# A fused stencil, attention, MLP and expert kernel: two sets of sums go to GpSimd, and the experts' response moves to other slots

## The chip, the cores and the metric

The kernel runs on one core of a Trainium2 chip. The time is that of the whole program on the device in microseconds; of several runs the median is given. All arithmetic is float32. In the rows of the profile PE is TensorE (PEld its weight loads), DVE is VectorE, ACT is ScalarE, POOL is GpSimd, and SP is the engine that issues nearly all DMAs.

## What is computed

The reference is a chain of four stages on x of shape (8, 512, 512), cut here to what matters:

```python
x = max(x + df(x, A_grid, B_grid) * dt, 0)                  # L0: a stencil on a 512x512 grid
x = layernorm(x) * (1 + scale) + shift                      # L1: attention with 16 heads ...
x = x + (softmax(q @ k.T + bias, mask) @ v @ Wo + bo)
h = layernorm(x) * g2 + beta2
x = x + gelu(h @ W1 + b1) @ W2 + b2                         # ... and an MLP, 512 -> 2048 -> 512
e = expert_idx[b]                                           # L2: one expert for each sample
r = x + gelu(x @ Wi[e] + bi[e]) @ Wo[e] + bo[e]
x = layernorm(r) * gamma[e] + beta[e]
basis = gram_schmidt(U) @ gram_schmidt(V).T                 # L3: a low-rank response with a gate
strength = sigmoid(relu(mean(x) @ w1.T + b1) @ w2.T + b2) * sigmoid(safety)
out = x + strength * ((x @ basis) @ basis.T[:, :32] @ resp_w.T + resp_b + safety_bias)
```

## The kernel before

The grid stage and the attention take the first 1078 us and aren't touched. `mlp_stage` follows. It makes sixteen passes q = 0 to 15: q = 0 to 7 are the MLP of L1 for one sample each, q = 8 to 15 the expert of L2 for one sample each, with L3 for the sample before woven in. Each pass multiplies 512 rows by 512x2048 (layer 1, `wi`) and by 2048x512 (layer 2, `wo`).

**Two levels of Strassen-Winograd.** Every product is split in quadrants, and seven products of sums stand for eight. Layer 1 does so once: four groups g of the hidden units, seven products each (the table `L1`), from sums S1 to S4 of the weights (`w_quads`, GpSimd) and T1 to T4 of the features (`b_staged`, tiles `tb` and, in place, `bt`). They are used in the order B00, B10, T2, T3, T1, T4, B11. Layer 2 has seven products P1 to P7 of quarters of the activations (`act`, sums s1 to s4: `s13`, `s2`, `s4`) and of `wo` (sums t1 to t4: `t13`, `t2`, `t4`). P1 and P5 are taken whole (`second`, tile y). P2, P6, P7, P3 and P4 are split once more (`third`, tiles y_32a/b, y_40a/b, y_44a/b, y_48a/b and y_52a/b); their own sums are `l_sum` (left, from act, on DVE) and `r_sum` (right, from wo, on GpSimd).

**Slots.** A pass has 56 slots: four matmuls of 256 columns each in layer 1 (slots 0 to 27), in P1 (28 to 31) and in P5 (36 to 39), and seven matmuls of 128 columns in P2 (32 to 35), P6 (40 to 43), P7 (44 to 47), P3 (48 to 51) and P4 (52 to 55). The last pass has P3 ahead of P7. `at(hooks, s, f, ...)` puts a piece of work f in slot s; `go(s)` records it there. So hooks fix the order in which an engine's instructions stand, not their time: an engine runs ahead, or falls behind, as its inputs, its buffers and its own order let it. What is recorded through `pin` keeps the order of the program on its engine. The weight loads of `load_wi`, `load_wo`, `load_x` and `load_extra` go to SP's queue without `pin`, and a scheduler places them there; SP carries out its queue in order, and an issue that has to wait for a buffer holds up those behind it.

**Staging.** Where DVE would read both operands from SBUF, ACT first copies one of them to PSUM (`staged`, L1519 for one part and L1524 for two, tag "tr", two buffers); l_sum's parts are called p2a, p2b, p2c and so on. PSUM tiles of products have the tag "u" with six buffers, among them y, u, and po of the response.

**What the change touches**, with line numbers of the kernel before:

- `b_staged` (L1527), called in slot 51 for the next pass: T1, T2, T3 (in place of quadrant 01 of bt) and T4 on DVE, each in two halves of 128x256, with three staged copies of two halves each.
- `s4` and `s4_stage` (L1746, L1751): S4 = quadrant 01 of act minus S2, per group 128x512, on DVE from staged copies, in slots 38 to 40. S4 is the left side of P3 and overwrites the quadrant that P2 reads.
- `t4` (L1742): T4 of wo, on GpSimd, from slot 37 (q up to 8), 40 (q = 9 to 14) or 43 (q = 15). It is the right side of P4.
- the table of l_sum's and r_sum's slots (L1757): the columns are the name of the product, the slots of the left sums and the slots of the right sums.
- `add_beta` (L2079), for the sample o = q - 1, in slot 36: DVE adds strength times the response's bias to the row `beta` in place (L2081); then GpSimd adds that row to x, four adds of 128x512.
- `tail_sum` (L2085): the response's matmuls po, four of 512 columns with 32 rows each, in slot 46. `tail_add` (L2092): x += strength * po on DVE, in four slots; the output goes out after the second and the fourth.

Near it and unchanged: `load_extra` (L1391), in slot 45 for the next pass, loads that expert's rows, gamma and beta with two buffers each; the row of q + 1 takes the place of that of q - 1. `load_wi` (L1363) loads the next pass's first and second weight groups in slots 48 and 52, 1 MB each, into buffers that P7's and P3's sums have used. `gs_stage`, `gs_norm` and `gs_b` are a step of the Gram-Schmidt, in passes 0 to 8; the step at the end of passes 0 to 7 stands in slots 52, 53 and 55: DVE makes two dot products, GpSimd a root (gs_d), DVE updates the matrix (qm), and GpSimd issues two DMAs (qb<-qm, L1259).

Of the kernel before, what the change touches and what calls it, by code (L numbers as in the profile page):

```python
# [16 lines left out]
ALU = mybir.AluOpType  # L17
# [1180 lines left out]
def mlp_stage(tc, a, small, xp, io, wo8, x1d, ident, eidx, sigs, layernorm, rstd_of, phalf, wl3, g2, b1, first):  # L1198
    nc = tc.nc
    H = 256  # L1200
    NG = 4
    pin = tc.keep_in_program_order
    with ExitStack() as ctx:
# [12 lines left out]
        def add(out, x, y, op=ALU.add):  # L1216
            pin(nc.vector.tensor_tensor(out, x, y, op))  # L1217
# [9 lines left out]
        n = 2 * RK  # L1227
# [299 lines left out]
        def b_staged(q):  # L1527
            def b(i, k, j):
                v = bts[q][2 * i + k]
                return v[:, 2 * j : 2 * j + 2, :, :] if len(v.shape) == 4 else v[:, H * j : H * j + H]  # L1530

            t1, t2, t4 = (
                as_rows(ap.tile([P, 2, H], F32, name=f"tb{i}_{q}", tag=f"tb{i}", bufs=1), b(0, 0, 0))
                for i in range(3)
            )
            b01, b11 = (staged(f"b{i}1_{q}", b(i, 0, 1), b(i, 1, 1)) for i in range(2))
            for k in range(2):
                add(t1[k], b01[k], b(0, k, 0), ALU.subtract)
            for k in range(2):
                add(t2[k], b11[k], t1[k], ALU.subtract)  # L1540
            for k in range(2):
                add(b(0, k, 1), b11[k], b(0, k, 1), ALU.subtract)
            tbs[q] = {
                "B00": lambda k: b(0, k, 0), "B10": lambda k: b(1, k, 0),
                "B11": lambda k: b(1, k, 1), "T3": lambda k: b(0, k, 1),
                "T1": lambda k: t1[k], "T2": lambda k: t2[k],
                "T4": lambda k: t4[k],
            }
            b10 = staged(f"b10_{q}", b(1, 0, 0), b(1, 1, 0))

            def rest():
                for k in range(2):
                    add(t4[k], b10[k], t2[k], ALU.subtract)

            rest()

        def b_quads(q, hold=False):
            def b(i, k, j):
# [52 lines left out]
        def run(q, hooks):  # L1611
# [10 lines left out]
            def act_quad(g, i, j):  # L1622
                return acts[:, g, 2 * j : 2 * j + 2, H * i : H * i + H]

            def stage(key, src):
                st[key] = staged(f"{q}_{key}", src)

            st = {}
# [114 lines left out]
                o = quad(wo[:, g], 1, 0)  # L1743
                gadd(o, o, quad(wo[:, g], 0, 0), sub)

            def s4(*gs_):  # L1746
                for g in gs_:
                    o = act_quad(g, 0, 1)
                    add(o, st[f"s4_{g}"], act_quad(g, 0, 0), sub)

            def s4_stage(*gs_):  # L1751
                for g in gs_:
                    stage(f"s4_{g}", act_quad(g, 0, 1))

            tail, last = q > NB, q == NQ - 1
            four = (40, 41, 42), (44, 45, 46)
# [1 line left out]
                at(hooks, s, set_up, part)  # L1758
            for g in range(NG):
                at(hooks, 30 + g, t2, g)  # L1760
                at(hooks, (43 if last else 40 if tail else 37) + g, t4, g)
            for key, ss_, ts_ in (
                ("p2", (28, 29, 30), (23, 24, 25, 26) if q else (20, 21, 22, 23)),
                ("p6", (36, 37, 38), (33, 34, 35, 36)),
                ("s4", (), ()),
                ("p7", four[last], (28, 28, 29, 29) if tail else (19, 20, 21, 22) if q else (23, 24, 25, 26)),
                ("p3", four[not last], (43, 43, 44, 45) if tail and not last else (40, 41, 42, 43)),
                ("p4", (47, 48, 49), (46, 46, 47, 48) if tail else (44, 45, 46, 47)),
            ):
                if key == "s4":  # L1770
                    at(hooks, 30, stage, "s2_0", act_quad(0, 0, 0))
                    for g in range(NG):
                        at(hooks, 31 + g, s2, g)
                    at(hooks, 38, s4_stage, 0, 1)
                    at(hooks, 39, s4, 0, 1)
                    at(hooks, 39, s4_stage, 2, 3)
                    at(hooks, 40, s4, 2, 3)
                    continue
                if key == "p4" and last:
                    continue  # L1780
                for n_, s in enumerate(ss_):
                    at(hooks, s, l_sum, key, n_)
                for n_, s in enumerate(ts_):
                    at(hooks, s, r_sum, key, n_)
# [418 lines left out]
        def at(hooks, s, f, *args):  # L2203
            hooks.setdefault(s, []).append(lambda: f(*args))
# [8 lines left out]
        for q in range(NQ):  # L2213
            hooks = {}
            nx = q + 1 if q + 1 < NQ else None

            if q:
                at(hooks, 0, load_wi, q, 2)
                at(hooks, 0, load_wi, q, 3)
                at(hooks, 1, w_quads, q, 1, gadd)  # L2220
            at(hooks, 0, load_wo, q)
            if nx:
                if nx >= NB:
                    at(hooks, 45, load_extra, nx)
                at(hooks, 2, load_x, nx)
                at(hooks, 48, load_wi, nx, 0)
                at(hooks, 52, load_wi, nx, 1)
            if 1 <= q <= NB:
                at(hooks, 4, lambda q=q: nc.sync.dma_start(x2d[q - 1], xs[q - 1]))

            if q <= NB:
                done = 4 * q - 1 if q else 0
                rounds = [(5, 8)] if q == NB else [(5, 8), (13, 16), (21, 24), (52, 55)]
                if q == 0:
                    rounds = (6, 9), (14, 17), (52, 55)
                for i, (s, e) in enumerate(rounds):
                    at(hooks, s, gs_stage, done + i)
                    at(hooks, s + 1, gs_norm, done + i)
                    at(hooks, e, gs_b, done + i)
            for r in range(R):  # L2240
                at(hooks, (24 if q > NB else 9 if q else 10) + r, add_row, q, r)
            at(hooks, 8 if q else 7, w_quads, q, 2, gadd)
            at(hooks, 16 if q else 14, w_quads, q, 3, gadd)
            for g in range(NG):
                at(hooks, ((5, 6, 12, 13) if q else (10, 12, 17, 18))[g], t13, q, g)
            if nx:
                if nx < NB:
                    for h in range(2):
                        at(hooks, 17 + h if q else 19 + 2 * h, norm, nx, h)
                    for r in range(R):  # L2250
                        at(hooks, 33 + r, normed, nx, r)
                for r in range(R):
                    at(hooks, 34 + r, lambda r=r, n=nx: rows32(
                        n, r, hs[n, r] if n < NB else xs[n][:, r, :]
                    ))
                at(hooks, 38 if q <= NB else 40, turn, nx)
                if nx < NB:
                    for c in range(KC):
                        at(hooks, 46 + c, scale, nx, c)
                at(hooks, 51, b_staged, nx)  # L2260
                at(hooks, 51, w_quads, nx, 0, gadd)
            if q == 0:
                at(hooks, 1, gs_a, 0)
                at(hooks, 10, load_constants)
            if q == 1:
                at(hooks, 10, constants)
            if q == NB:
                for i, s in enumerate((10, 13, 15, 17, 20)):
                    at(hooks, s, low_rank, i)
            elif q > NB:  # L2270
                every = range(R)
                o = q - 1
                at(hooks, 5, tail_norm, o, every)
                at(hooks, 9, tail_normed, o)
                for r in range(R):
                    at(hooks, 11 + r, lambda r=r, o=o: rows32(o, r, xs[o][:, r, :]))
                at(hooks, 15, tail_spread, o)
                at(hooks, 18, tail_gamma, o, every)
                for c in range(KC):
                    at(hooks, 20 + c, tail_scale, o, c)  # L2280
                at(hooks, 25, tail_feats, o, every)
                at(hooks, 26, gate, o)
                at(hooks, 32, strength, o)
                at(hooks, 35, guarded, o)
                at(hooks, 36, add_beta, o)
                for r in range(R):
                    at(hooks, 46, tail_sum, o, r)
                    at(hooks, ((47, 49, 53, 54) if nx else (47, 48, 49, 51))[r], tail_add, o, r)
            if q == NQ - 1:
                half = range(0, 2)  # L2290
                at(hooks, 49, tail_norm, q, half)
                at(hooks, 50, tail_normed, q)
                for c in range(KC):
                    at(hooks, 52 + c, tail_turn, q, half, [c])
                at(hooks, 55, last_affine, 0)
            run(q, hooks)


# [86 lines left out]
```

## Time and profile before

| | |
|---|---|
| median of 3 runs | 2631.25 us (2630.48 to 2633.49) |
| the profiled execution | 2631.78 us; its span 2630.0 us, granted TensorE clock 0.994 |
| busy in the span | PE 98%, DVE 79%, POOL 66%, ACT 52% |
| pass q = 3, 1362.66 to 1456.08 | 93.42 us; PE busy throughout, DVE 77.40, POOL 72.34, ACT 40.90 |
| pass q = 10, 2025.42 to 2122.99 | 97.57 us; PE busy 97.26, DVE 74.67, POOL 71.45, ACT 42.95 |
| one add of 128x512 on POOL | 1277 ns |
| the same on DVE, one operand in PSUM | 680 ns, the next starts 600 ns after it |

How to read it: a pass begins with its first matmul u<-bt,wi. Line L1217 is every add of DVE in this stage and L1220 every one of POOL, so groups are told apart by their tiles: "act<-act,st_p4a" is P4's S3, "yw<-y_48a,yw" the evacuation of P3's first half, "x<-y_44b,x" the addition of P7 to x. A line of the waits names who waited, for whom, the sum of the waits, how often, and the longest. A line of the timeline gives start, duration, engine, line, operation, tiles, count, and in brackets the idle time of the engine ahead of it with what ended it.

### The profile page before, as it was taken

The page shows a single profiled execution, that of the slowest core. Times are in us where ns is not written, and L with a number is a line of the kernel's source. Part 1 is how long each engine was busy: PE and PEld are TensorE (multiplying, and loading weights), DVE is VectorE, ACT ScalarE, POOL GpSimd, SP SyncE. Part 2 cuts the span into 40 slices and gives each one's busy share as a digit, 9 for nine tenths or more (in the row PEclk, how much of TensorE's full clock was granted, in tenths as well). Part 3 has the DMA queues.
Part 4 walks back from the last instruction along what each step waited for, and adds up shares of the span by engine and source line. Part 5 has one row for each costly group of instructions (what it writes and reads, how often), then busy time and mean ns, then how long its engine had stood idle before and what let it go on. Part 6 is the DMA issues. An engine that isn't in the chain of part 4 may idle for free. (4 is left out here: it accounts for less than half of the span.)

```text
span 2630.0 us, 45403 instructions
## 1 busy us (share of the span) xinstructions
PE 2584.8 (98%) x16048; PEld 1967.7 (75%) x16048; DVE 2081.1 (79%) x4116; ACT 1366.7 (52%) x2871; POOL 1734.7 (66%) x1422
## 2 busy tenths in 40 slices
PE   6999999999999999999999999999999999999998
PEld 3455555555555555798899899899899989989887
DVE  7978898978888756588888888788778778777777
ACT  2676767677767766244344344343443543544443
POOL 4555565655555656378778777877767777777774
PEclk9999999999999999999999999999999999999999
DMA  8765757666767556443653653465345265255250
GB/s 325 259 225 189 256 194 249 211 220 226 248 212 250 178 158 203 143 148 79 175 181 60 164 197 100 105 190 154 100 168 186 89 207 191 82 201 196 77 177 33
DMA packets 242135, 460.69 MB, mean 175 GB/s; under 512 B 33936, under 2 KB 77528, under 8 KB 232822
## 3 DMA queue, kind: packets, MB, share of 16 engines
q1 hardware_dynamic: 238042, 447.04, 49.9%
q0 software_dynamic: 3552, 10.72, 4.2%
q8 instruction: 128, 2.10, 0.3%
q14 instruction: 97, 0.79, 0.1%
q10 hardware_dynamic: 316, 0.03, 0.0%
HBM read 398.43 MB, written 55.09 MB: 172 GB/s over the span
## 5 line engine op out<-in xcount | busy, mean ns | idle before, releaser
L998 POOL TENSOR_TENSOR bt<-bt,mk 128x1024 f32<-128x1024 f32 x256 | 542.0, 2142 | 59.0 <-DMA bt<-in_bias 37.6
L1026 ACT ACTIVATE bt<-bt,mn 128x512 f32<-128x512 f32 x512 | 365.8, 718 | 78.5 <-DVE mn L1021 78.3
L564 PEld LDWEIGHTS tr<-ident,bt 128*128 128x128 f32 x2048 | 229.6, 141 | 149.4 <-issue 102.4
L1021 DVE CUSTOM_DVE_ANT_0 bt<-s,bt 128x512 f32<-128x512 f32 x512 | 329.8, 683 | 4.3 <-PE s L561 3.6
L1211 PE MATMUL u<-bt,wi 128*128 128x256 f32 x1440 | 330.8, 379 | 0.0
L1052 ACT COPY pt<-tr 128x512 f32<-128x512 f32 x376 | 207.9, 584 | 209.2 <-PE tr L564 201.8
L1211 PEld LDWEIGHTS u<-bt,wi 128*128 128x128 f32 x1440 | 272.3, 190 | 36.4
L564 PE MATMUL tr<-ident,bt 128*128 128x128 f32 x2048 | 276.6, 277 | 7.5 <-ACT pt L1052 2.9
L1217 DVE TENSOR_TENSOR act<-u,u 128x512 f32<-128x512 f32 x256 | 172.6, 682 | 123.2 <-PE u L1211 70.8
L1211 PE MATMUL u<-tb,ws 128*128 128x256 f32 x1024 | 242.7, 380 | 0.0
L1220 POOL TENSOR_TENSOR wo<-wo 128x512 f32<-128x512 f32 x175 | 221.1, 1277 | 8.7
L1211 PEld LDWEIGHTS u<-tb,ws 128*128 128x128 f32 x1024 | 193.9, 190 | 27.7 <-DVE x L1217 1.4
L1050 DVE COPY pt<-tr 128x512 f32<-128x512 f32 x136 | 93.7, 689 | 140.5 <-PE tr L564 140.0
L1796 ACT ACTIVATE act<-act,bi 128x512 f32<-128x512 f32 x128 | 83.6, 711 | 222.7 <-DVE act L1217 222.6
L1796 ACT ACTIVATE act<-act,b 128x512 f32<-128x512 f32 x128 | 83.6, 711 | 192.8 <-DVE act L1217 192.8
L561 PE MATMUL s<-kt,qt 32*128 32x512 f32 x1024 | 167.5, 643 | 1.2 <-ACT kt L651 0.8
L1220 POOL TENSOR_TENSOR q<-wo 128x512 f32<-128x512 f32 x96 | 121.7, 1278 | 49.8 <-PE pf L1211 32.5
L1217 DVE TENSOR_TENSOR u<-u,u 128x512 f32<-128x512 f32 x192 | 130.5, 680 | 28.9 <-PE u L1211 28.3
L1220 POOL TENSOR_TENSOR ws<-wi 128x512 f32<-128x512 f32 x60 | 76.7, 1278 | 91.7 <-DMA wi<-in_W 49.9
L561 PE MATMUL ctx<-pt,v 128*32 128x256 f32 x2048 | 128.7, 390 | 0.0
L561 PEld LDWEIGHTS ctx<-pt,v 128*32 128x32 f32 x2048 | 63.0, 111 | 83.0 <-issue 49.3
L1220 POOL TENSOR_TENSOR q<-wo,q 128x512 f32<-128x512 f32 x96 | 122.6, 1277 | 2.7
(473 smaller groups left out, 5909.9 us busy)
## 6 DMA issues: line engine op xcount, KB each, us to landing
bt<-in_bias SPq DMA_DIRECT2D x256, 512.0 KB
wo<-in_W SPq DMA_DIRECT2D x32, 1024.0 KB
wi<-in_Wi SPq DMA_DIRECT2D x32, 1024.0 KB
wo<-in_Wo_e SPq DMA_DIRECT2D x32, 1024.0 KB
wi<-in_W SPq DMA_DIRECT2D x28, 1024.0 KB
td<-tt SPq DMA_DIRECT2D x22, 1024.0 KB
bt<-td SPq DMA_DIRECT2D x120, 128.0 KB
gq<-coef_q SPq DMA_DIRECT2D x21, 512.0 KB
```

Of the source, the lines that this page charges most:

```text
L561: pin(nc.tensor.matmul(out, lhsT=lhsT, rhs=rhs, start=start, stop=stop))
L564: pin(nc.tensor.transpose(out, src, ident))
L998: nc.gpsimd.tensor_tensor(bt, bt, mask[b, r][:, None, :].to_broadcast([P, 2, S]), ALU.add)
L1021: nc.vector.tensor_tensor_reduce(bt[:, i, :], ss[h], bt[:, i, :], -1.0, 3.0e38, ALU.add, ALU.min, mn)
L1026: nc.scalar.activation(bt[:, i, :], bt[:, i, :], AF.Exp, bias=mn, scale=-1.0, accum_out=sums[b, c][:, h, r : r + 1],)
L1050: pin(nc.vector.tensor_copy(pt[:, :, r % 2, :], tr))
L1052: pin(nc.scalar.copy(pt[:, :, r % 2, :], tr))
L1211: pin(nc.tensor.matmul(out, lhsT=lhsT, rhs=rhs, start=start, stop=stop))
L1217: pin(nc.vector.tensor_tensor(out, x, y, op))
L1220: pin(nc.gpsimd.tensor_tensor(out, x, y, op))
L1796: nc.scalar.activation(acts[:, g, k, :], acts[:, g, k, :], func, bias=bi[:, j : j + 1])
```

## The change

S4 is made on GpSimd, in place and without staging, one group in each of the slots 37 to 40 (36 to 39 in the last pass). The staging copies of S4 go. T4 of wo moves to slots 43 to 46 (45 to 48 in the last pass). P4's left sums move one slot forward, and some right sums of P3 and P4 in passes after 8 to other slots. The sums T3 and T4 of the next pass's features leave DVE: they are made on GpSimd in slot 55 from SBUF, and their staged copy goes. From q = 9 to 14 add_beta moves from slot 36 to 49, the four matmuls of tail_sum from 46 to 51, and tail_add from 47, 49, 53, 54 to 52, 53, 54, 55. In the last pass add_beta moves from 36 to 42.

```diff
 b_staged:
-            for k in range(2):
-                add(b(0, k, 1), b11[k], b(0, k, 1), ALU.subtract)
...
-            b10 = staged(f"b10_{q}", b(1, 0, 0), b(1, 1, 0))
 
             def rest():
                 for k in range(2):
-                    add(t4[k], b10[k], t2[k], ALU.subtract)
-
-            rest()
+                    gadd(b(0, k, 1), b(1, k, 1), b(0, k, 1), ALU.subtract)
+                for k in range(2):
+                    gadd(t4[k], b(1, k, 0), t2[k], ALU.subtract)
+
+            late[q] = rest
 run:
-            def s4(*gs_):
-                for g in gs_:
-                    o = act_quad(g, 0, 1)
-                    add(o, st[f"s4_{g}"], act_quad(g, 0, 0), sub)
-
-            def s4_stage(*gs_):
-                for g in gs_:
-                    stage(f"s4_{g}", act_quad(g, 0, 1))
+            def s4(g):
+                o = act_quad(g, 0, 1)
+                gadd(o, o, act_quad(g, 0, 0), sub)
...
-                at(hooks, (43 if last else 40 if tail else 37) + g, t4, g)
+                at(hooks, (36 if last else 37) + g, s4, g)
...
-                ("p3", four[not last], (43, 43, 44, 45) if tail and not last else (40, 41, 42, 43)),
-                ("p4", (47, 48, 49), (46, 46, 47, 48) if tail else (44, 45, 46, 47)),
+                ("p3", four[not last], (40, 40, 41, 42) if last else (40, 41, 42, 43)),
+                ("t4", (), ()),
+                ("p4", (46, 47, 48), (46, 46, 47, 48)),
...
-                    at(hooks, 38, s4_stage, 0, 1)
-                    at(hooks, 39, s4, 0, 1)
-                    at(hooks, 39, s4_stage, 2, 3)
-                    at(hooks, 40, s4, 2, 3)
+                if key == "t4":
+                    for g in range(NG):
+                        at(hooks, (45 if last else 43) + g, t4, g)
                     continue
 the passes:
                 at(hooks, 51, w_quads, nx, 0, gadd)
+                at(hooks, 55, lambda n=nx: late.pop(n)())
...
-                at(hooks, 36, add_beta, o)
+                at(hooks, 49 if nx else 42, add_beta, o)
                 for r in range(R):
-                    at(hooks, 46, tail_sum, o, r)
-                    at(hooks, ((47, 49, 53, 54) if nx else (47, 48, 49, 51))[r], tail_add, o, r)
+                    at(hooks, 51 if nx else 46, tail_sum, o, r)
+                    at(hooks, ((52, 53, 54, 55) if nx else (47, 48, 49, 51))[r], tail_add, o, r)
```

More of the change, by code (lines that the diff above doesn't have):

```diff
@@ L1548, in b_staged @@
             }
-            b10 = staged(f"b10_{q}", b(1, 0, 0), b(1, 1, 0))
             def rest():
                 for k in range(2):
-                    add(t4[k], b10[k], t2[k], ALU.subtract)
-            rest()
+                    gadd(b(0, k, 1), b(1, k, 1), b(0, k, 1), ALU.subtract)
+                for k in range(2):
+                    gadd(t4[k], b(1, k, 0), t2[k], ALU.subtract)
+            late[q] = rest
+        late = {}
         def b_quads(q, hold=False):
@@ L1764, in run @@
                 ("p6", (36, 37, 38), (33, 34, 35, 36)),
-                ("s4", (), ()),
+                ("s2", (), ()),
                 ("p7", four[last], (28, 28, 29, 29) if tail else (19, 20, 21, 22) if q else (23, 24, 25, 26)),
-                ("p3", four[not last], (43, 43, 44, 45) if tail and not last else (40, 41, 42, 43)),
-                ("p4", (47, 48, 49), (46, 46, 47, 48) if tail else (44, 45, 46, 47)),
+                ("p3", four[not last], (40, 40, 41, 42) if last else (40, 41, 42, 43)),
+                ("t4", (), ()),
+                ("p4", (46, 47, 48), (46, 46, 47, 48)),
             ):
-                if key == "s4":
+                if key == "s2":
                     at(hooks, 30, stage, "s2_0", act_quad(0, 0, 0))
@@ L1773, in run @@
                         at(hooks, 31 + g, s2, g)
-                    at(hooks, 38, s4_stage, 0, 1)
-                    at(hooks, 39, s4, 0, 1)
-                    at(hooks, 39, s4_stage, 2, 3)
-                    at(hooks, 40, s4, 2, 3)
+                    continue
+                if key == "t4":
+                    for g in range(NG):
+                        at(hooks, (45 if last else 43) + g, t4, g)
                     continue
```

## The prediction

> **What bounds the kernel.** I read the page's engine table first, then who waited for whom on PE, then the same for the DMA queue on SP, then the order of time of one pass.
>
> ```profile
> span 2630.0 us, 45403 instructions
> ...
> PE 2584.8 (98%) x16048; PEld 1967.7 (75%) x16048; DVE 2081.1 (79%) x4116; ACT 1366.7 (52%) x2871; POOL 1734.7 (66%) x1422
> ```
>
> PE is busy for all but 45 us. The waits of PE from 1000 us on (the last attention rows and all sixteen passes) show what is left to win:
>
> ```profile
> PE y_52a L1211 <- DVE act L1217: 2.6, 4, 0.8
> PE y_48a L1211 <- DVE yw L1217: 2.4, 7, 0.6
> PE y L1211 <- ACT act L1796: 0.8, 1, 0.8
> ```
>
> Only the first two touch what is moved. So no more than about 5 us (0.2%) can be won, while a new wait costs its length in each pass where it stands. A pass is 93.42 us in the first half (q = 2 to 4, no loss) and 97.57 us for q = 9 to 14. I work out one pass of each kind, in offsets (+) from its first layer-1 product: q = 3 from 1362.66 and q = 10 from 2025.42.
>
> **First half, q = 0 to 7.** S4 on GpSimd: 4 adds at 1.277 us, 5.1 us, in place of 4 staging copies (ACT) and 4 adds (DVE, one each 0.60 us). POOL comes to them at +62.8, P2 has been read by +61.5, so they end at +68.0; P3's sums are staged at about +77.6 on ACT. Hidden, with 9 us to spare. T4, which they displace, moves back 10.2 us to +78.1 and P4's sums to +83.2; P4 starts at +87.2. POOL has the room: it stands idle for 8.22 us before the next weights' sums.
>
> DVE's four S4 adds were behind P6's sums; without them DVE reaches the end of P6's product early and waits for PE: its addition to x ends at +77.0 instead of +77.9. P4's first sum now goes ahead of y_44b's evacuation and S3 is there at +84.4 (it was +87.7; PE wants it at +88.1): the y_52a waits go, **-2.6**.
>
> T3 and T4 of the next features leave DVE (4 x 0.33 = 1.3 us, there with PSUM copies) and go to the end of POOL's queue, behind the Gram-Schmidt DMAs that wait for DVE's qm. qm ended at +97.90; I get +96.28 (0.3 from the lead above, 1.3 from the sums gone). The DMAs start 0.53 later, as before, and take 1.03: T3 starts at +97.87. A POOL add of 128x256 isn't in the trace. Bounds: 0.64 us (half of 128x512 at 1.277) and 0.845 (the line through 1.277 and the 2.142 of 128x1024). I take 0.74, the line from 128x1 at 0.196 to 1.277. Halves at +98.6 and +99.3; PE's fourth product wants them at 93.42 + 3 x 1.727 = +98.60 and +99.03. A wait of 0.35 in six passes: **+2.1** (bounds 0.5 and 4; if DVE wins nothing, 1.9 us x 7 = 13). T4 is wanted 3.5 us after T3: no cost. POOL's lag of 1.7 us afterwards delays the last GELU by about as much as PE is delayed plus its slack of 1.3: no cost.
>
> [...]
>
> **Passes q = 9 to 14.** Here add_beta moves from slot 36 to 49, the quarter sums from 46 to 51. The load of the next expert's beta row (load_extra, slot 45) takes the buffer of the row that add_beta reads: two buffers, and the row of q+1 replaces that of q-1. In the built program's order this load still stands on SP's queue ahead of the next pass's first weights, and waits for the fourth POOL add of add_beta. That wait already exists:
>
> ```profile
> SPq L1368 <- PE y_44b L1211: 34.5, 6, 6.2
> ...
> SPq L1398 <- POOL x L1220: 23.5, 6, 3.9
> ```
>
> Today it is free, because SP then waits up to 6.2 us for wi's buffer anyway. SP and POOL in q = 10:
>
> ```profile
> 2097.37 0.33 SPq L1398 DMA_DIRECT2D beta<-in_beta  x1
> 2097.89 1.33 SPq L1402 DMA_DIRECT2D cols<-in_gamma  x1
> 2099.41 0.38 SPq L1402 DMA_DIRECT2D cols<-in_beta  x1
> ...
> 2103.70 0.43 SPq L1409 DMA_DIRECT2D x<-x2d  x1
> 2110.13 0.40 SPq L1368 DMA_DIRECT2D wi<-in_Wi  x1
> ```
>
> ```profile
> 2092.38 4.97 POOL L1220 TENSOR_TENSOR x<-x,beta 128x512 f32<-128x512 f32 x4 [4.24 <-DVE beta L2081]
> ...
> 2115.28 1.27 POOL L1220 TENSOR_TENSOR ws<-wi 128x512 f32<-128x512 f32 x1 [1.40 <-DMA wi<-in_Wi]
> ```
>
> The reader is to see: the adds end at 2097.35, the beta load goes out at 2097.37; wi goes out at 2110.13 and is there at 2115.28, 5.15 us later. PE wants it at 2122.99, so 7.7 us are spare. In the new order nothing but the two cols loads lies between beta and wi: 2.6 us from the end of add_beta (2097.35 to 2099.79, and 0.15 to the next issue). So wi lands 2.6 + 5.15 = 7.75 after add_beta's end.
>
> When is that? DVE's rows:
>
> ```profile
> 2103.33 0.57 DVE L1217 TENSOR_TENSOR y_40b<-y_40b,yw 128x384 f32<-128x384 f32 x1 [0.39 <-ACT y_40b L1886]
> 2103.93 0.70 DVE L1217 TENSOR_TENSOR y_40b<-y_40b,yu 128x512 f32<-128x512 f32 x1
> 2104.66 0.69 DVE L1217 TENSOR_TENSOR x<-y_40b,x 128x512 f32<-128x512 f32 x1
> 2106.61 0.69 DVE L1217 TENSOR_TENSOR q<-st_p3a,act 128x512 f32<-128x512 f32 x1 [1.25 <-ACT st_p3a L1519]
> ```
>
> P6 ends at +77.0. ACT's copy 0.47 and the three adds 2.0: +79.5; wait for P3's staging 1.25: +80.75; P3's sums 2.67: +83.4; ACT stages P4's first two parts and yw_44: 0.85; yw_44 1.06: +85.35; P4's first two sums 1.3: +86.6; ACT stages the third and copies y_44b: 0.85; y_44b and x 2.6: +90.05; P4's other sums 1.4: +91.45; beta 0.65: +92.1; POOL (idle since P4's sums, about +84.5) 4.97: **+97.1**, where it was +71.9. wi lands at +104.85; the next pass starts there and not at +97.57: **+7.35 a pass**. P4 itself starts late too: y_52a takes y_48a's PSUM bank, freed by yw_48 behind beta at +93.1, against +91.3 now; it ends at +99.5 and lies under the wait for wi.
>
> POOL's first sums start at the landing: 4 take 5.09 (2115.28 to 2120.37), then T3's halves: first at 5.88 and second at 6.6 after the landing; PE wants them at 5.18 and, delayed, 6.3: **+1.0 a pass** (0.75 to 1.2). It shifts the rest of that pass with it.
>
> [...] beta (two SBUF inputs) took 707 ns with POOL idle. [...]
>
> **Last pass.** Its y_48a wait of 0.55 (DVE free of S4) goes: -0.5.
>
> **Sum**, against the profiled execution, 2631.78 us (0.5 above the median): -2.6 + 2.1 + 6 x (7.35 + 1.0) - 0.5 = +49.1, so **2681**. Open sizes: wi's landing may take the second weight load's 6.15 (issued about 0.6 after others: 2116.13 to 2122.28), +6; the first cols load may be shorter alone, -6; DVE and ACT may interleave 1.5 us better, -9; T3 in the first half, -2 to +11. Range 2662 to 2700.
>
> **Rivals.** (a) *Only the PSUM bank counts*: SP gets wi out in time, for instance because it isn't held by the beta row, and only y_52a is late: 1.9 us x 6 = 11.4, less 1.0 for the rest, 2642. Against: the order on SP and the 23.5 us of waits for that very release. (b) *The first half suffers too*: DVE wins nothing and T3 comes 1.9 us late: 2681 + 11 = 2692. For: DVE has waited for ACT's copies all along the stretch. (c) *Not slower*: add_beta ends early. The deciding point: its end + 7.75 must not pass +97.5, so before +89.8. Then no new wait stands in the experts' passes and both old ones go: -2.6 - 2.4 + 2.1, 2629. For: DVE loses 2.4 us of S4 and 1.3 of T3/T4 ahead of it. Against: the chain above waits for PE's P6 end, which swallows all but 0.4, and 7.3 us are missing.
>
> **Chances.** Forecast 0.80, (a) 0.07, (b) 0.09, (c) 0.04. Less than 0.2% (5.3 us) is about what a measurement of this kernel can't tell from no change: (c) is mostly there, and 0.01 of it beyond; the rest is slower. So faster 0.01, same 0.03, slower 0.96. The range holds the forecast and (b), and leaves out (a) and (c).
>
> **What would show it.** Right: each pass from q = 9 to 14 some 106 us instead of 97.57; PE's first layer-1 product waits for DMA wi by 5 to 6 us, six times; SP's wait for POOL x near 15 us or more each; PE u waits for POOL bt about 0.7; no y_52a wait in q = 0 to 7. Wrong: a wi load issued before the beta row, add_beta ending before +90, or passes under 100 us; first-half passes over 95 us would make it (b).

## The result and the profile after

The change makes the kernel slower: 2695.55 us (median of 6 runs, 2693.91 to 2699.36) against 2632.26 us for the kernel before in runs beside it, a ratio of 1.0242 (95% interval 1.0229 to 1.0256). The profiled execution took 2699.36 us, 67.6 more than that of before. The first lines of its page:

```profile
span 2697.5 us, 45440 instructions
...
PE 2616.8 (97%) x16048; PEld 1985.9 (74%) x16048; DVE 2031.1 (75%) x3992; ACT 1322.0 (49%) x2777; POOL 1855.6 (69%) x1546
```

Two things are to be seen. PE's idle time (span less busy) grew from 45.2 to 80.7 us, so 35.5 us are waits. And PE is busy 32.0 us longer with the same 16048 matmuls: part of them ran slower. The waits of PE from 1000 us on, which of before were y_52a, y_48a and y:

```profile
PE u L1211 <- DMA wi<-in_Wi: 27.6, 5, 6.3
PE po L1211 <- DVE x L1217: 5.8, 6, 1.0
PE u L1211 <- issue: 4.8, 1, 4.8
PE qtr L1214 <- DVE qm L1289: 2.5, 1, 2.5
```

The y_52a and y_48a waits are gone. In their place PE waits six times for the next pass's first weights ("issue" is the sixth), six times for the bank of a response tile, and once, in pass 8, for the Gram-Schmidt matrix. Pass by pass in the two profiled executions, from one first layer-1 product to the next (us; that of the change is the slowest of its six runs, 3.8 us above their median):

| pass | before | after | difference | predicted |
|---|---|---|---|---|
| up to q = 0 | 1078.32 | 1077.32 | -1.0 | 0 |
| q = 0 to 7 together | 752.95 | 751.37 | -1.6 | -0.5 |
| q = 8 | 96.58 | 102.07 | +5.5 | 0 |
| q = 9 | 97.58 | 105.88 | +8.3 | +8.35 |
| q = 10 to 14, mean | 97.57 | 108.32 | +10.75 | +8.35 |
| q = 15 to the end | 110.16 | 112.65 | +2.5 | -0.5 |

That q = 9 agrees so well with its prediction is partly luck: two errors of 1.0 us cancel in it (below). The chain that makes q = 9 to 14 long is the predicted one. GpSimd and SP at the end of q = 10 (the pass starts at 2036.65):

```profile
2131.11 4.96 POOL L1220 TENSOR_TENSOR x<-x,beta 128x512 f32<-128x512 f32 x4 [7.63 <-DVE beta L2078]
2144.88 1.26 POOL L1220 TENSOR_TENSOR ws<-wi 128x512 f32<-128x512 f32 x1 [8.81 <-DMA wi<-in_Wi]
```

```profile
2114.01 0.43 SPq L1409 DMA_DIRECT2D x<-x2d  x1
2136.10 0.36 SPq L1398 DMA_DIRECT2D beta<-in_beta  x1
2136.64 0.39 SPq L1402 DMA_DIRECT2D cols<-in_gamma  x1
2137.22 0.38 SPq L1402 DMA_DIRECT2D cols<-in_beta  x1
2137.84 1.00 SPq L1368 DMA_DIRECT2D wi<-in_Wi  x2
2138.95 1.03 SPq L2097 DMA_DIRECT2D out<-x  x2
```

SP issues nothing for 22 us, from 2114 to 2136. The row of beta goes out 0.03 us after the last of add_beta's four adds (2136.07), the weights 1.74 later, and they are there at 2144.88. PE over the same stretch:

```profile
2127.09 1.13 PE L1211 MATMUL po<-rw,ft 32*128 32x512 f32 x6
2129.20 1.11 PE L1211 MATMUL po<-rw,ft 32*128 32x512 f32 x2 [0.97 <-DVE x L1217]
...
2145.16 6.39 PE L1211 MATMUL u<-bt,wi 128*128 128x256 f32 x16 [5.28 <-DMA wi<-in_Wi]
```

PE is idle for 5.28 us, and then its first 16 matmuls take 6.39 us; before they took 3.62. The clock granted in these windows (the figure after the times of the five engines; 1.00 is full speed) tells why:

```profile
2129.00:2130.00 1.00, 0.81 (x2) 0.29 (x2) 0.97 (x3) 0.32 (x1) 0.00 (x0) 1.00 0.00 0
2131.00:2133.00 2.00, 2.00 (x12) 2.00 (x11) 1.93 (x8) 0.19 (x1) 1.89 (x2) 0.50 0.00 0
2141.00:2143.00 2.00, 0.00 (x0) 0.00 (x0) 0.56 (x1) 0.00 (x0) 0.00 (x0) 1.00 0.91 351
2145.20:2148.00 2.80, 2.80 (x7) 2.26 (x8) 0.00 (x0) 0.00 (x0) 2.72 (x3) 0.50 1.07 391
...
2152.00:2156.00 4.00, 4.00 (x20) 3.51 (x20) 1.73 (x3) 0.00 (x0) 3.92 (x4) 1.00 1.05 387
```

The clock is still 1.00 while PE waits at 2141 to 2143, is 0.50 when it starts again, and 1.00 from 2152 on. It is 0.50 too at 2131 to 2133, after the 0.97 us wait of the response. Before, the clock was 1.00 in all these passes.

### The profile page after: what moved, and what is told of

The parts are those of the page before. It is cut to its first block, busy times and chain, and to the rows that moved or that the text cites. A ratio compares the mean times of both kernels' runs of the same rounds, so it can differ in the third digit from the quotient of the medians.

```text
span 2697.5 us, 45440 instructions
## 1 busy us (share of the span) xinstructions
PE 2616.8 (97%) x16048; PEld 1985.9 (74%) x16048; DVE 2031.1 (75%) x3992; ACT 1322.0 (49%) x2777; POOL 1855.6 (69%) x1546
## 4 chain that ended last, share of the span: by engine, by line
PE 47%; DVE 4%; DMA 1%; POOL 1%; ACT 1%; issue 1%; SPq 0%; DVEq 0%; ACTq 0%; POOLq 0%
PE u L1211 26%; PE y L1211 8%; PE y_32a L1211 2%; PE y_40a L1211 2%; PE y_40b L1211 1%; PE y_32b L1211 1%; DMA wi<-in_Wi 1%; PE y_52a L1211 1%; PE y_48a L1211 1%; PE y_44a L1211 1%; POOL x L1220 1%; PE y_48b L1211 1%; PE y_52b L1211 1%; PE y_44b L1211 1%; DVE x L1217 1%
## 5 line engine op out<-in xcount | busy, mean ns | idle before, releaser
L1211 PE MATMUL u<-bt,wi 128*128 128x256 f32 x1440 | 350.0, 394 | 32.4 <-DMA wi<-in_Wi 27.6
L1211 PEld LDWEIGHTS u<-bt,wi 128*128 128x128 f32 x1440 | 282.5, 198 | 79.1 <-issue 33.4
```

Of the source, the lines that this page charges most:

```text
L1211: pin(nc.tensor.matmul(out, lhsT=lhsT, rhs=rhs, start=start, stop=stop))
```

## The experiments

**1. The response back.** The whole change, with add_beta, tail_sum and tail_add at their old slots.

```diff
-                at(hooks, 49 if nx else 42, add_beta, o)
+                at(hooks, 36, add_beta, o)
...
-                    at(hooks, 51 if nx else 46, tail_sum, o, r)
+                    at(hooks, 46, tail_sum, o, r)
```

> The changed kernel with the response (add_beta, tail_sum, tail_add) back in its old slots; S4 and T3/T4 stay on GpSimd. Theory (the beta row's load holds SP, so the experts' first weights are late): the six waits of PE for wi go, and passes 9 to 14 come back to 97.5 to 99.5 us. The first half keeps its -1.6 us, pass 8 its +5.5 us, and y_48a's wait may grow from 0.3 to 0.8, since P4's staging now stands ahead of yw_44 on ACT: 2636 to 2644 us. Rival (the load on GpSimd is what makes the passes late): PE still waits in passes 9 to 14 and the time stays above 2670 us.

Measured: 2638.9 us, ratio 1.0032 (1.0019 to 1.0045). No wait for wi is left; q = 9 to 14 take 98.05. So nearly all of the loss is the response's, and a rest of 0.3% belongs to what is left of the change: 2.4 us in pass 8, 3.5 in the last pass and 0.5 in each of q = 9 to 14. (Experiment 8 shows that the last two come from the slots of P4's left sums and of add_beta beside S4, not from the moves to GpSimd as such.)

**2. The response alone.** The kernel before, with the response at the new slots.

```diff
-                at(hooks, 36, add_beta, o)
+                at(hooks, 49 if nx else 42, add_beta, o)
...
-                    at(hooks, 46, tail_sum, o, r)
+                    at(hooks, 51 if nx else 46, tail_sum, o, r)
```

> The kernel before with only the response's slots changed; S4 and T3/T4 stay on DVE. Theory: DVE reaches beta about as late as in the changed kernel, SP is held, and six passes lose 10 to 11 us each: 2688 to 2698 us, with PE waiting for wi. Rival (GpSimd's added sums are needed for the loss): under 2645 us.

Measured: 2682.44 us, ratio 1.0183 (1.016 to 1.0205). PE's waits:

```profile
PE u L1211 <- DMA wi<-in_Wi: 21.7, 5, 4.6
PE y_52a L1211 <- DVE yw L1217: 5.7, 6, 1.0
PE u L1211 <- issue: 4.9, 1, 4.9
```

The wait for wi comes without S4, T3 or T4. The time is some 6 us under what was expected: in q = 10 the four adds end 96.0 us after the pass's start, where they end 99.4 after it in the whole change, and less half clock is granted. In q = 9, at full clock in both, they end 94.4 and 97.0 us after it. So taking S4, T3 and T4 off DVE did not make add_beta earlier: in the whole change all four of P4's left sums stand ahead of beta on DVE, here two of them, and DVE waits 0.85 us twice for ACT's copies of y_44a and y_44b, here only 0.39 for the second. Of the 50 us, the passes q = 9 to 14 take 44, and the last pass 4.9.

**3. The beta row behind the weights.** The whole change, with the row of beta loaded by itself in slot 53, after both weight loads; nothing else moves.

```diff
-            for n_, bufs in (("bo_e", 1), ("gamma", 2), ("beta", 2)):
+            for n_, bufs in (("bo_e", 1), ("gamma", 2)):
...
+                if nx >= NB:
+                    at(hooks, 53, load_beta, nx)
```

> The changed kernel, but the load of the beta row alone is taken out of load_extra and issued in slot 53, behind both weight loads. add_beta and the sums stay where the change put them. Theory: wi is there in time; what is left in passes 9 to 14 is y_52a's late bank (about 1.9 us) and up to 1.7 us of half clock after short waits: passes of 99 to 101 us, 2640 to 2652 us in all. Rival (the bank and DVE's order, not the load, hold the pass): passes stay over 105 us and the time over 2680 us.

Measured: 2644.97 us, ratio 1.0047 (1.0031 to 1.0063). Five of the six passes take 99.43 us, and of the waits of q = 9 to 14 one kind is left:

```profile
PE po L1211 <- DVE x L1217: 5.9, 6, 1.0
```

Same instructions, same late add_beta: only that the row no longer stands ahead of the weights on SP. Some 50 us go. This is the mechanism of the forecast, isolated. What stays, 99.43 against 97.10 in experiment 9, is rival (a)'s kind of wait, on the PSUM bank of the fourth response tile rather than on y_52a's.

**4. Junk in the wait.** The whole change; in q = 10 to 15, PE multiplies features by the identity twelve times ahead of the first product (into a bank that the product then overwrites), so that it is busy while it waits.

```diff
+                    for _ in range(12 if q > NB + 1 and g + m == 0 else 0):
+                        mm(as_rows(u, B(0))[0], ident, B(0), True, True)
```

> The changed kernel with 12 extra matmuls of 128x256 (identity times bt, their result is overwritten) ahead of the first product of passes 10 to 15, in PE's wait for wi; the output is the same. In the changed kernel the 16 records after that wait took 6.2 to 6.4 us where 3.6 is usual, at a granted clock of 0.50. Clock theory (the clock is halved for some microseconds because PE stood idle): the granted clock stays at 1.00, the first product takes its 1.73 us, PE then waits 0.7 to 1.0 for POOL's T3, and 1.5 to 2.4 us a pass are won: 2681 to 2687 us against 2695.5. Rival (the slowness comes from the DMA traffic or from cold weights, not from idleness): the first product is as slow as before and the time is 2693 to 2699 us.

Measured: 2687.63 us, ratio 1.0207 (1.0182 to 1.0232): 8 us less than the change, for 12 more matmuls a pass. The start of q = 11:

```profile
2136.12 5.35 PE L1211 MATMUL u<-bt,ident 128*128 128x256 f32 x24
2142.14 3.72 PE L1211 MATMUL u<-bt,wi 128*128 128x256 f32 x16 [0.68 <-DMA wi<-in_Wi]
2145.70 1.89 PE L1211 MATMUL u<-tb,ws 128*128 128x256 f32 x8
2147.97 2.24 PE L1211 MATMUL u<-bt,wi 128*128 128x256 f32 x8 [0.38 <-POOL bt L1220]
```

The 16 matmuls take 3.72 us again and no pass starts at half clock; and now the T3 wait that the forecast had (0.38) is there. Four of the passes q = 10 to 14, with the junk, take 106.2 to 106.6 us, the fifth 108.1. The time came 0.6 us above what was expected; 3.4 us of half clock still follow the response's wait in five of the six passes.

**5. S4 alone.** S4 on GpSimd with T4's and the sums' new slots; T3 and T4 on DVE, the response at its old slots. That is experiment 1 with `b_staged` of the kernel before.

```diff
+            for k in range(2):
+                add(b(0, k, 1), b11[k], b(0, k, 1), ALU.subtract)
...
-                    gadd(t4[k], b(1, k, 0), t2[k], ALU.subtract)
+                    add(t4[k], b10[k], t2[k], ALU.subtract)
```

> S4 on GpSimd with the new slots of T4 and of P3's and P4's sums, but T3 and T4 of the features back on DVE and the response at its old slots. Theory (what remains of the loss with the response at its old slots comes from T3 and T4 of the features): the wait inside the fourth product goes, passes 2 to 4 take 93.43 us again, pass 8 about 96.6, no y_52a wait in q = 0 to 7; passes 9 to 14 some 97.6 to 97.9; only the last pass keeps its 3.5 us, since add_beta in slot 36 still stands ahead of S4 and of P3's sums there. 2632 to 2636 us. Rival (S4 itself delays what follows on GpSimd): passes stay at 93.83 and 98.05 and the time at 2637 to 2640.

Measured: 2636.5 us, ratio 1.0018 (1.0009 to 1.0027), between the two. Half right: q = 1 to 7 take 93.43 each without any loss, better than before, so S4 on GpSimd costs nothing there and T3's lateness was the 0.4 us a pass. But passes 9 to 14 stay at 98.05, and pass 8 takes 100.77: these two are not T3's and T4's.

**6. T3 and T4 alone.** The kernel before with only T3 and T4 on GpSimd in slot 55.

```diff
-                    add(t4[k], b10[k], t2[k], ALU.subtract)
+                    gadd(t4[k], b(1, k, 0), t2[k], ALU.subtract)
...
+                at(hooks, 55, lambda n=nx: late.pop(n)())
```

> The kernel before with only T3 and T4 of the next features on GpSimd in slot 55. Theory: with S4 still on DVE the Gram-Schmidt's qm ends later than in the whole change, so the fourth product waits 0.4 to 1.0 us in each pass of the first half, pass 8 waits for qm by 2.5 us or more, and the y_52a waits stay: 2637 to 2645 us. Rival (T3 and T4 are free, the loss is S4's): 2630 to 2633.

Measured: 2637.84 us, ratio 1.0028 (1.0016 to 1.004).

```profile
PE y_48a L1211 <- DVE yw L1217: 2.9, 7, 0.7
PE y_52a L1211 <- DVE act L1217: 2.2, 4, 0.8
PE u L1211 <- POOL bt L1220: 2.1, 7, 0.3
PE qtr L1214 <- DVE qm L1289: 1.5, 1, 1.5
```

T3 starts 4.84 us after the pass's start in q = 3, where it is 4.45 in the whole change, and passes 2 to 4 take 94.6 us. The two moves help each other: without S4 gone from DVE, T3 is later. The wait for qm was 1.5, less than expected.

**7. Pass 8's features on DVE.** The whole change, but T3 and T4 of that one pass as before.

```diff
+            if q == NB:
+                for k in range(2):
+                    add(b(0, k, 1), b11[k], b(0, k, 1), ALU.subtract)
...
+                late[q] = lambda: None
+                return
```

> The whole change, but T3 and T4 of pass 8's features are made on DVE from staged copies as before (one of fifteen feature sets). Theory (GpSimd, late by T3 and T4, delays the Gram-Schmidt root and so qm in pass 8, and PE's wait of 2.5 us brings the half clock): pass 8 back from 102.07 to 96.6 to 97.3 us, the qtr wait near 0.4, no half clock in pass 8, everything else as in the whole change: 2689 to 2692 us. Rival (the wait for qm comes from S4 or from DVE's own order): pass 8 stays at 102, 2694 to 2697.

Measured: 2694.42 us, ratio 1.0246 (1.023 to 1.0262). The theory falls: pass 8 takes 100.08 us and still waits 2.3 us for qm. The trace shows what it missed. The last Gram-Schmidt row is a DMA that GpSimd issues, and ACT's copy of it starts the chain to qm. ACT's row before, and after:

```profile
1841.66 0.58 ACT L1519 COPY st_qb<-qb 64x512 f32<-64x512 f32 x1 [7.84 <-DMA qb<-qm]
```

```profile
1840.68 0.58 ACT L1519 COPY st_qb<-qb 64x512 f32<-64x512 f32 x1 [9.40 <-DMA qb<-qm]
```

The issues begin at 1834.63 and 1831.99, 3.37 and 3.29 us after the pass's start; the copy follows 7.0 and 8.7 us later. Over the kernels this time varies from 6.8 (experiment 9) to 9.0 us (experiment 6); why isn't shown. To it come GpSimd's lag (its two roots start 1.4 and 1.1 us after DVE's sums, 0.2 and 0.1 in the kernel before) or, in experiments 5, 7 and 8, an issue 1.2 us later. In the whole change it is GpSimd's lag that decides: in experiment 3 the row is copied 0.7 us sooner after the pass's start, but the first root starts 14.70 us after it all the same, and PE waits the same 2.49 us. Without that lag the later issue makes nearly the same wait. Most of the 2.0 us that pass 8 wins here is half clock: 3.4 us of it instead of 6.8.

**8. S4 alone, tuned.** Experiment 5 with P4's left sums in slot 47 from q = 9 to 14, and add_beta in slot 42 in the last pass.

```diff
-                ("p4", (46, 47, 48), (46, 46, 47, 48)),
+                ("p4", (47, 48, 49) if tail else (46, 47, 48), (46, 46, 47, 48)),
...
-                at(hooks, 36, add_beta, o)
+                at(hooks, 36 if nx else 42, add_beta, o)
```

> S4 alone on GpSimd as in the first of these, with P4's left sums in slot 47 again in passes 9 to 14 and add_beta in slot 42 in the last pass. Theory: the y_48a waits of passes 9 to 14 go back to 0.3 us or less (DVE frees the bank of y_44 ahead of P4's sums), the last pass loses the wait of y_44a for GpSimd and takes about 109.4; 2627 to 2631 us, so up to 0.2% under the kernel before. Rival (the waits move to y_52a in those passes): 2631 to 2635.

Measured: 2624.84 us, ratio 0.9977 (0.9967 to 0.9986), faster than the kernel before. Passes 9 to 14 take 97.10 with no wait, and the last 108.89. In experiment 5 DVE's row for y_44a has an idle time that it lacks here (2106.21, no bracket):

```profile
2111.16 1.07 DVE L1217 TENSOR_TENSOR yw<-y_44a,yw 128x128 f32<-128x128 f32 x3 [0.85 <-ACT yw L1878]
```

With P4's sums in slot 46, their two staging copies stand ahead of the copy of y_44a on ACT; DVE waits 0.85 us for it, frees the bank late, and PE waits 0.8 at y_48a.

**9 and 10. The low-rank product later.** Experiment 8, and the whole change, with the steps in pass 8 that PE takes part in moved from slots 13, 15, 17, 20.

```diff
-                for i, s in enumerate((10, 13, 15, 17, 20)):
+                for i, s in enumerate((10, 17, 19, 21, 24)):
```

> The tuned S4 version with the four matmul steps of the low-rank product in pass 8 put at slots 17, 19, 21 and 24 instead of 13, 15, 17 and 20 (the qtr transposes are what PE waits with). Theory (in pass 8 the last Gram-Schmidt row comes late, by its transfer's landing and by GpSimd's and DVE's queues, and PE stands before it in slot 13): no qtr wait, pass 8 falls from 99.5 to 96.2 to 97.0 us; 2621 to 2623 us. Rival (ACT's GELU, queued behind the copy of that row, is late too and PE waits for it next): pass 8 stays above 98.5, 2624 to 2626.

> The whole change with the same later slots of the low-rank product in pass 8. Theory: the wait of 2.5 us and the half clock after it go, pass 8 falls from 102.07 to 96.2 to 97.5 us, the rest as in the whole change: 2688 to 2692 us. Rival (the row's lateness reaches PE by another way, ACT's GELU or DVE's queue): pass 8 above 99 and 2693 to 2697.

Measured: 2622.59 us, ratio 0.9971 (0.996 to 0.9983), and 2694.35 us, ratio 1.0245 (1.0231 to 1.0259). Pass 8 falls to 96.41 and 97.54 us. In the second the profiled span is 5.0 us shorter than that of the change, though its median is only 1.2 lower and 2 us over what was expected, so there the pass, not the total, carries the verdict. The first is the fastest version found, 0.29% under the kernel before. Its waits from 1000 to 2600 us, in which nothing of the sixteen passes is left but pg, a small product of the low-rank steps in pass 8:

```profile
PE tr L564 <- DVE pt L1050: 0.5, 1, 0.5
PE tr L564 <- ACT pt L1052: 0.5, 1, 0.5
PE s L561 <- DVE mn L1021: 0.4, 2, 0.2
PE pg L1211 <- DVE qd L1295: 0.2, 1, 0.2
```

**11 and 12. What makes the weights land late.** The whole change: the two cols loads put ahead of the row of beta; or the second weight load put behind the stores of the output.

```diff
...
+                    at(hooks, 44, load_cols, nx)
                     at(hooks, 45, load_extra, nx)
```

> The whole change, with the two cols loads put ahead of the beta row on SP's queue, so that they no longer stand between its wait for add_beta and the first weight load. The weight load landed 7.04 us after its issue in the whole change and 5.15 before. Theory A (the transfers issued behind it, the second weight load and the stores of the output, take the transfer engines from it): issue comes 1.2 us earlier, landing stays near 7.0, passes 9 to 14 lose 1.2 us less each, 2686 to 2690 us. Theory B (the cols loads, of many small pieces, hold the engines ahead of it): landing falls to 6 us or less as well, 2678 to 2684 us.

```diff
-                at(hooks, 52, load_wi, nx, 1)
+                if nx <= NB + 1:
+                    at(hooks, 52, load_wi, nx, 1)
...
+            if nx and nx > NB + 1:
+                at(hooks, 55, load_wi, nx, 1)
```

> The whole change, with the second weight load of passes 10 to 15 issued behind the two stores of the output instead of directly behind the first weight load. Theory A (what is issued within 0.6 us behind the first load shares the engines with it): its landing falls from 7.04 to 5.6 to 6.5 us, passes 9 to 14 lose 0.5 to 1.4 us less each, 2686 to 2692 us. Theory B (the cols loads ahead of it): landing 7.0 us and 2693 to 2697 us as before.

Measured: 2688.04 us (1.0212, 1.0195 to 1.0229) and 2700.45 us (1.026, 1.0243 to 1.0277). With cols ahead, the weights go out 0.62 us after add_beta instead of 1.77, and land 6.8 to 7.4 us after their issue: the gain is the issue, not the landing. With the second load behind, they land after 6.8 to 7.2 us and the time is above both forecasts: nothing gained, and this form of theory A falls.

Theory B's forecast (a landing after 6 us or less) failed in the first, but the DMA packets of the change speak for its mechanism. From 2138 to 2141, just after the issue at 2137.84, 1060 of 1141 packets are under 512 B (the two cols loads go in pieces of 4 bytes), and 57 GB/s are moved; from 2141 to 2144.4 it is 372 GB/s. So the weights run at that rate only some 3.5 us after their issue, behind cols; before, with nothing just ahead, it was some 2 us (issue at 2110.13; 82 GB/s from 2111 to 2112, 340 in the next us, 416 in the one after). With cols ahead of the row, the first 3 us are slow without them (111 GB/s from 2132 to 2135), with the row of beta alone just ahead, and the rest takes longer, beside the second load and the stores. So some 1.5 of the 1.9 us by which the landing is later than before fall into the time in which the cols pieces run. Why nothing is won without them, the row of beta or what follows, stays open.

## Why the prediction was right, and where it was off

The time lies inside the range, 14.5 us above the predicted value, on the predicted side and by the predicted mechanism (experiments 1, 2 and 3). In the profiled executions the sum is 18.4 us short: 12 in q = 10 to 14, 5.5 in pass 8 and 3.0 in the last pass, less 2 that were won ahead of them. (The sum has a slip: 104.85 less 97.57 is 7.28 and not 7.35, 0.4 us in all.)

- **Where add_beta ends.** Predicted +97.1; in q = 9, which starts at full clock, 2027.78 less 1930.77, or +97.0.
- **From its end to the weights.** Predicted 7.75 (2.6 + 5.15); measured 8.8 (1.77 to the issue, 7.04 to the landing). The first cols load took 0.39 alone and not 1.33, as the open sizes allowed; the landing is the mis-sized term, 1.9 us longer where they allowed 1.0. Net +1.0 a pass. With it q = 9 should take 97.0 + 8.8 = 105.8; it took 105.88. The forecast came to the same only because it counted 1.0 for T3, which cost nothing there.
- **Half clock: the step that was missing.** From q = 10 on, every pass starts after an idle PE, and the clock stays at 0.50 for 3.4 or 6.8 us from shortly before the wait's end: 4.75 us of q = 10 at half clock is 2.4 us lost. The whole chain to add_beta starts later by it (99.4 against 97.0). The mean of q = 10 to 14 is 2.4 over q = 9, and pass by pass the excess follows the clock: half of the time at half clock at the start of q = 10 to 14 is 2.4, 2.7, 3.1, 1.6 and 2.5 us, the excess over q = 9 is 2.6, 2.7, 2.9, 1.5 and 2.5. The wait makes PE slow, and that makes the next wait as long again; nothing is caught up. Experiment 4 takes it away, and the passes fall to about 106.3. The last pass begins the same way, hence its +2.5.
- **T3 in q = 9 to 14.** Predicted 1.0 a pass: in the change it is 0, since PE at half clock reaches the fourth product late; in experiment 4, where q = 10 to 15 start at full clock, the product behind T3's comes 0.3 to 1.0 us late, of which the list of waits shows 0.38 twice. A cost that a larger one covers.
- **The first half.** Predicted -2.6 and +2.1; measured -1.6 together. The y_52a waits are gone. T3 started at +4.45 as worked out, and cost 0.40 (0.35 predicted), which the list of waits doesn't show: it lies inside a group, whose eight matmuls take 2.24 us instead of 1.89 in q = 3:

```profile
1364.68 2.24 PE L1211 MATMUL u<-bt,wi 128*128 128x256 f32 x8
```

  One GpSimd add of 128x256 took 0.73 us on the mean (a pair 1.41); the forecast took 0.74.
- **"POOL's lag of 1.7 us afterwards ... no cost": wrong in pass 8.** I looked at who waits for the lag among the GELUs, not at the root of the Gram-Schmidt behind it on the same engine. PE waits 2.48 instead of 0.36 for qm, and 3.4 us are lost to half clock after it: 5.5. The half clock does not always come with it: with the same wait pass 8 takes 99.0 us in experiments 1, 3, 4 and 11, where the clock stays full, so 2.4 us are lost without it. And the lag is not the only thing that can make the wait: experiment 7 removes it, and 2.3 us of waiting stay. Experiments 9 and 10 show what takes the wait away: PE's steps in later slots.
- **The row of beta on DVE** took 741 ns, with GpSimd idle for 7.63 us ahead of its sums as the forecast had it (before, the seven rows took 707 to 741 ns, 708 at the median).
- **Hidden, as predicted:** the late PSUM bank. It showed at po, not y_52a, and lies under the wait for wi; experiment 3 uncovers it at 2.3 us a pass.
- **The rivals.** (a) would be a kernel in which SP doesn't hold the weights: experiment 3 is that kernel, at 2645 where 2642 was worked out. (b) is out: q = 2 to 4 took 93.83. (c) failed on add_beta's end, 7 us behind its deciding point.

## What to carry to other kernels

Before moving a read of a small buffer to a later place, look for the load that refills that buffer and for what stands behind it in its queue: here one row of 512 numbers held up 1 MB of weights, and loading it behind them instead gave back 50 us. Then read a new wait of TensorE with the clock beside it, since the matmuls after the wait can cost half as much again as the wait (2.77 us more on 16 of them, after 5.28 of waiting). And test the halves of a combined change alone: a version with S4 on GpSimd, the staging order mended, add_beta in slot 42 of the last pass and the low-rank product out of the way is 0.29% faster than the kernel before; the response's move hid it. How much of that is S4's alone no run shows.

## What the runs showed of the hardware

- After idle stretches of PE the granted clock was 0.50 for 3.4 or 6.8 us. In the change it followed each of the six waits for wi, but also waits of 0.97 us at the response, in four of six passes of the change and in one of six in experiment 3. The length of a wait alone does not decide: the wait of 2.5 us in pass 8 was followed by 6.8 us of half clock in the change, by 3.4 in experiment 12 and by none in experiments 1, 3, 4 and 11.
- The response's matmuls, of 32 rows each and each tile on other rows, ran beside one another: one po record lasts 0.59 to 0.69 us (experiment 9), and all eight took 1.07 us to the next instruction (2103.11 to 2104.18 in experiment 8). When the fourth tile waited, its two alone took 1.03 us (2119.97 to 2121.00 in experiment 3), after 1.1 for the other six. A late fourth tile cost its wait and its company.
